# A two-layer spectral and convolutional network on one core: a new order list for the stretch without convolution, and a small column fix-up split into a load and an arithmetic part

## The chip, the core and the metric

The kernel runs on one core of a Trainium2 chip. The core has five engines that matter here: TensorE (PE in the profile; its weight loads are PEld), VectorE (DVE), ScalarE (ACT), GpSimd (POOL) and SyncE (SP), which here only issues DMA transfers. Each engine works through its own queue in order; semaphores tie the queues together. The metric is device time in microseconds (us). Three runs of the kernel before took 4526.14, 4532.66 and 4543.19 us; the profiled run took 4532.45 us, with a span of 4530.7 us from first to last instruction.

## What is computed

The input is `x` of shape (4, 256, 256, 64). Layer 0 does this for each of the four images:

```
h   = layernorm(x) @ w_te + b_te                     # 64 -> 128 channels
F   = fft2(h)                                        # over the 256 x 256 positions
fc  = gelu(concat(real F, imag F) @ w_fc + b_fc)     # 256 -> 256 channels, at each frequency
sp  = real(ifft2(fc[:128] + i fc[128:]))
x1  = x + sp @ w_tp + b_tp
h2  = layernorm(x1) @ w_fe + b_fe
out = x1 + gelu(depthwise_conv3x3(h2, w_dw) + b_dw) @ w_fp + b_fp
```

Layer 1 adds a moving average over the first axis to a filtered spectrum; in the kernel it is a product with one 256 x 256 matrix for each channel. Everything is fp32.

## The kernel before, in words

The forward and inverse Fourier transforms are products with cosine and sine tables. `forward_h` transforms the rows h of the image in chunks of two columns and their mirror images, and writes the result to DRAM (`y_d`). `spectral` transforms along w, mixes channels, applies gelu, projects back and transforms back along w, writing to DRAM (`u_d`). `convolution` transforms back along h, adds the residual, normalises, does the 3x3 convolution by rows and writes `x_d`. A last stage multiplies by layer 1's matrices.

These parts overlap. On TensorE, VectorE, ScalarE and GpSimd the order of instructions is written out by hand: `period(n)` walks a list of short operation names, and `do(op, index)` first does what `FOLLOWS` says must come before. A name with `:-1` means the operation of one index earlier. There are two lists:

- `SPECTRUM`, for periods without convolution: n = 35 to 70, 36 periods, while the first image's spectrum is made.
- `FULL`, for the periods with convolution: n = 71 to 204. Convolution of the four images begins at n = 71, 104, 136 and 169.

One period of `SPECTRUM` handles one forward chunk, two pairs of spectral blocks and one backward step. What the letters are (line numbers are those of the profile):

- forward, one each: `fl` load `xt` (L374 to L379); `fq` squares on ScalarE (L328); `fr`, `fm` two reductions on VectorE (L331, L338); `fR`, `fM` two small VectorE steps (L335, L342); `fp` a power on GpSimd, `rstd` (L348); `fx` scaling on GpSimd (L355); `fa`, `fb` two add/subtract pairs on VectorE (`xb` L392, `xt` L412); `fh0`, `fh1` on GpSimd (`xb` L417); `y0`, `y1` matmuls (L423) with evictions `yt0`, `yt1` on ScalarE (L441). `xb` has one buffer, and `fa` follows both `y` of the chunk before.
- spectral, one for each pair: `x` matmuls (L528) and copy `xs` (L543); `m0`, `m1` mixing matmuls (L552), each into two PSUM banks; `gc0`, `gc1` copy the second bank (L566); `b0`, `b1` add and subtract, reading the first bank (VectorE, L571); `g0`, `g1` gelu on ScalarE (L575); `p0`, `p1` fold on GpSimd (L581); `z` matmuls (L605) and copy `zs` (L613); `w` transposes (L622) and copy `zt` (L632).
- backward, one each: `u` matmuls (L654), `us` copy (L671), `uc` (VectorE, L684 and L685), `uf` (VectorE, L716 in even and L703 in odd steps), then a store to `u_d` (L692).
- convolution: `c0`, `s`, `r0`, `r1`, the statistics `cq` to `cp`, and others. `cm` and `cM` are two statistics steps on VectorE and `cp` a power on GpSimd (L348).
- `cc`, `other_columns`: once for each image it reads the columns w = 0 of `u_d`, does nine small VectorE operations (L785 to L797) and writes three corrected columns to DRAM (`fix_d`). `load_u` (L761, L764) reads them eight periods later and more.

All matmul results go through one pool of eight PSUM banks, which are taken in turn in program order: the ninth taking waits until the first bank's reader is done. A period of `SPECTRUM` takes 18 banks. The tile `sq`, in which `fq` and `cq` leave their squares, has one buffer, and `cc` uses that buffer too. DMA transfers are all issued by SyncE in program order.

Of the kernel before, what the change touches and what calls it, by code (L numbers as in the profile page):

```python
# [11 lines left out]
F32 = mybir.dt.float32  # L12
AF = mybir.ActivationFunctionType
ALU = mybir.AluOpType
# [4 lines left out]
P = 128  # L19
N = 256  # L20
C = 64
# [108 lines left out]
def conv_seq_kernel(ctx: ExitStack, tc: tile.TileContext, a: dict, tables: bass.AP, out: bass.AP):  # L130
    nc = tc.nc
    x = a["x"]
# [4 lines left out]
    shared = ctx.enter_context(tc.tile_pool(name="shared", bufs=1))  # L137
# [6 lines left out]
    def column(ap):  # L144
        return ap.rearrange("(p o) -> p o", o=1)
# [47 lines left out]
    with tc.tile_pool(name="prep", bufs=1) as prep:  # L193

        def load(shape, name, src):
            t = prep.tile(shape, F32, tag=name, name=name)
            nc.sync.dma_start(t, src)
            return t

        w_te = load([C, HID], "w_te", a["w_te"])  # L200
        g1 = load([C, 1], "g1", column(a["g1"]))
        b1 = load([C, 1], "b1", column(a["b1"]))
# [155 lines left out]
    y_ds, u_ds = {}, {}  # L358
# [377 lines left out]
    def convolution(pool):  # L736
# [7 lines left out]
        name = lambda j: f"c_{j[0]}_{j[1]}"  # L744

        fixed, firsts = {}, {}
# [22 lines left out]
        def first_column(j):  # L769
            if j[1] == 0:  # L770
                col = ucs[j][:, 0]
                nc.vector.tensor_tensor(col, col, firsts.pop(j)[:, ::-1], ALU.add)

        def other_columns(j):

            b, q = j
            if q:
                return
            fixed[b] = spill.tile([P, 3, 2, C], F32, tag="fix_d", name=f"fix_d_{b}")
            v = shared.tile([P, 8, 2, C], F32, tag="sq", name=f"fix_{b}")  # L780
            for i in range(2):
                nc.sync.dma_start(v[:, 2 * i : 2 * i + 2], u_ds[b][i][:, :, 0])
            swapped = lambda t: t[:, ::-1]
            tt = nc.vector.tensor_tensor
            tt(v[:, 4], v[:, 2], swapped(v[:, 3]), ALU.add)  # L785
            tt(v[:, 5], v[:, 0], swapped(v[:, 1]), ALU.subtract)
            tt(v[:, 6], v[:, 2], swapped(v[:, 3]), ALU.subtract)
            total, diff = v[:, 0], v[:, 1]
            tt(total, v[:, 5], v[:, 6], ALU.add)
            tt(diff, v[:, 5], v[:, 6], ALU.subtract)  # L790

            tt(v[:, 3, 0], diff[:, 1], total[:, 0], ALU.subtract)
            tt(v[:, 3, 1], diff[:, 0], total[:, 1], ALU.add)
            nc.vector.scalar_tensor_tensor(
                v[:, 5, 0], total[:, 0], -1.0, diff[:, 1], ALU.mult, ALU.subtract
            )
            tt(v[:, 5, 1], total[:, 1], diff[:, 0], ALU.subtract)  # L797
            nc.sync.dma_start(fixed[b], v[:, 3:6])

        def load_x(j):  # L800
            b, q = j
# [40 lines left out]
        tt = pool.tile([P, NP, N + 2], F32, tag="tt", name="tt", bufs=1)  # L842
# [182 lines left out]
        def when(f, is_first):  # L1025
            return lambda j: f(j) if (j[1] == 0) == is_first else None
# [4 lines left out]
            "UL": when(load_u, True),  # L1031
            "XL": when(load_x, True),
            "c0": first_column,
            "cc": other_columns,
            "s": back_h,
            "r0": residual_even,
# [155 lines left out]
    for b in range(B):  # L1192
# [9 lines left out]
        fh0 fb | fh1 fb | y0 fh0 fh1 | y1 fh0 fh1 | yt0 y0 | yt1 y1  # L1202
        xs x m0:-2 m1:-2 | m0 xs | m1 xs | gc0 m0 z:-2 | gc1 m1 z:-2 | b0 gc0 | b1 gc1 | g0 b0 | g1 b1
        p0 g0 | p1 g1 | z p0 p1 | zs z w:-1 | w zs | zt w | us u uc:-1 | uc us uf:-1 | uf uc
        s ul UL c0 | r0 s xl XL | r1 r0 | cq r1 | cr r1 | cR cr | cm cq | cM cm cR | cp cM
        cx cp t0:-1 t1:-1 | t0 cx | t1 cx | tt0 t0 T0:-1 T1:-1 | tt1 t1 T0:-1 T1:-1
        T0 tt0 tt1 eh:-2 | T1 tt0 tt1 gh:-2 | gm T1 | gh gm T1:1 | em T0 | eh em T0:1
        gc_0 gh o1:-2 | gc_1 gh o1:-2 | cf0 gc_0 | cf1 gc_1 | ce0 eh cf0 cf1 | ce1 ce0 | cE ce1
# [4 lines left out]
    def numbered(text):  # L1213

        return [(w.split(":")[0], int(w.split(":")[1]) if ":" in w else 0) for w in text.split()]

    follows = {}
    for line in FOLLOWS.replace("\n", "|").split("|"):
# [4 lines left out]

    FULL = numbered("""
        c0 s cf0:-3 cf1:-3 b0:-1 b1:-1 r0 r1 fx:-1 g0:-1 z:-2 zs:-2 x xs g1:-1 p0:-1 p1:-1
        o0:-4 fs0:-4 o1:-4 fs1:-4 ul:1 cq cr cR cm cM cp t0:-1 tt0:-1 t1:-1 tt1:-1 w:-2 zt:-2
        cx em:-3 eh:-3 T1:-1 T0:-1 fq fr fR fm fM fp m0 gc0 m1 gc1 ce0:-3 ce1:-3 cE:-3
        u us b0 b1 uc z:-1 zs:-1 x:1 xs:1 y0:-2 y1:-2 yt0:-2 yt1:-2 fl:1 a0:-3 a1:-3
        fa:-1 fb:-1 fh0:-1 fh1:-1 ft0:-4 ft1:-4 st0:-4 st1:-4 xl:1 cc w:-1 zt:-1 uf
        g0 g1 p0 p1 gm:-2 gh:-2 gc_0:-2 gc_1:-2 m0:1 gc0:1 m1:1 gc1:1 UL:1 XL:1  # L1230
    """)

    SPECTRUM = numbered("""
        fl:1 p0:-2 fq x z:-2 fr g0:-1 b1:-1 y0:-2 fx:-1 zs:-2 w:-2 fm xs g1:-1 m0 yt1:-2 zt:-2 fa:-1
        m1 u gc1 fR gc0 p0:-1 yt0:-2 fb:-1 us b1 fM p1:-1 b0 x:1 g1 fh1:-1 z:-1 fh0:-1 xs:1 m0:1
        zs:-1 uc gc0:1 w:-1 uf g0 m1:1 zt:-1 b0:1 fp y1:-1 gc1:1 p1
        UL:1 XL:1
    """)
    PAIRS = set("x xs m0 m1 gc0 gc1 b0 b1 g0 g1 p0 p1 z zs w zt".split())
# [45 lines left out]
    with in_order, ExitStack() as right:  # L1285
        with (
            tc.tile_pool(name="fwd", bufs=2, side="left") as fwd,
            tc.tile_pool(name="mix", bufs=2, side="left") as mixing,
        ):
            forward = forward_h(fwd)  # L1290
            load_group, begin, spectrum = spectral(mixing)
            ops |= forward
            do("fl", 0)
            with tc.tile_pool(name="matrices", bufs=2, side="right") as pool:
                m = matrices(pool)
                for n in range(S0):
                    starting(n, m)
                m[1]()
                load_group(0)
                begin(0)  # L1300
            ops |= spectrum
            conv = right.enter_context(tc.tile_pool(name="conv", bufs=2, side="right"))
            ops |= convolution(conv)
            for n in range(S0, S0 + opened(B - 1) + 2):
                period(n)
# [53 lines left out]
```

## Time and profile before

The stages below are from the profile's table of windows; busy times in each window of 100 or 200 us are given as shares of it.

| stretch, us | what runs | PE busy | DVE busy | POOL busy | ACT busy |
|---|---|---|---|---|---|
| 100 to 300 | forward alone, layer 1's matrices | 100% | 74% | 82% | 35% |
| 400 to 800 | the `SPECTRUM` list | 86 to 87% | 98 to 99% | 83 to 85% | 81 to 82% |
| 800 to 1000 | change to `FULL`, image 0 | 80, 86% | 93, 90% | 80, 83% | 71, 58% |
| 1000 to 1700 | the `FULL` list | 100% | 94 to 96% | 78 to 81% | 66 to 69% |
| 1800 to 1900 | change to image 1 | 92% | 92% | 74% | 61% |
| 2600 to 2800 | change to image 2, forward done | 100% | 79% | 54% | 63% |
| 3400 to 3600 | change to image 3 | 95% | 76% | 47% | 39% |
| 4000 to 4530 | end of convolution, layer 1 | 95% | 25% | 3% | 21% |

A busy share by itself doesn't say what a stage waits for; the groups of instructions, the waits and the timeline of the stage do.

### The profile page before, as it was taken

The numbers are of one execution on the slowest core, as the hardware profiler recorded it, in microseconds if no ns is written. First come the engines' busy times: TensorE is split into PE (matmuls) and PEld (weight loads), VectorE is DVE, ScalarE is ACT, GpSimd is POOL, SyncE is SP. The second block draws the span as 40 slices with busy tenths as digits, with TensorE's granted clock in tenths as the row PEclk, the third lists the DMA queues.
The fourth block names the chain that finished last, engine by engine and source line by source line (L and its number), as shares of the span: only waits on it lengthen the run. The fifth ranks groups of instructions, "written<-read, shape, count | busy, mean of one in ns | idle before, by whom it ended". The sixth has DMA issues, their size and how long they took to land.

```text
span 4530.7 us, 63718 instructions
## 1 busy us (share of the span) xinstructions
PE 4348.9 (96%) x22347; PEld 2227.3 (49%) x22347; DVE 3595.4 (79%) x5451; ACT 2506.6 (55%) x3686; POOL 2773.2 (61%) x1806
## 2 busy tenths in 40 slices
PE   7998888889999999999999999999999999999999
PEld 4543333345555555455555555555555455554444
DVE  6778999989999999999999777777777788862222
ACT  2337888666666666666666666666664333331111
POOL 5887888788888777787777555555554555530000
PEclk9999999999999999999999999999999999999999
DMA  5665555434444444444444343333334333328897
GB/s 172 203 191 152 141 144 148 139 105 131 131 131 133 137 127 135 124 135 135 137 137 117 94 117 98 99 107 94 104 107 144 100 101 94 103 89 321 318 327 266
DMA packets 756583, 655.02 MB, mean 145 GB/s; under 512 B 40141, under 2 KB 649375, under 8 KB 747944
## 3 DMA queue, kind: packets, MB, share of 16 engines
q1 hardware_dynamic: 756264, 650.95, 47.6%
q8 instruction: 179, 2.93, 0.3%
q14 instruction: 140, 1.15, 0.1%
HBM read 364.81 MB, written 286.00 MB: 144 GB/s over the span
## 4 chain that ended last, share of the span: by engine, by line
PE 76%; DVE 8%; POOL 4%; issue 2%; DMA 2%; SPq 0%; ACT 0%; POOLq 0%; DVEq 0%; ACTq 0%
PE ps_h_c L897 19%; PE ps_h_c L916 11%; PE ps_o L1156 9%; PE ps_p L552 7%; PE ps_f_c L972 5%; PE ps_s_c L814 4%; PE ps_z L605 4%; PE ps_u L654 4%; PE ps_x L528 4%; PE ps_t_c L851 3%; PE ps_ft_c L993 3%; DVE xb L392 2%; PE ps_y L423 2%; PE ps_zt L622 2%; DVE g L571 2%
## 5 line engine op out<-in xcount | busy, mean ns | idle before, releaser
L581 POOL TENSOR_TENSOR g<-g 128x512 f32<-128x512 f32 (+1 forms) x520 | 710.6, 1377 | 511.7 <-ACT g L575 511.6
L897 PE MATMUL ps_h_c<-td_c,wc_main 128*128 128x512 f32 x2048 | 923.7, 594 | 5.2 <-DVE h_c L942 5.2
L571 DVE TENSOR_TENSOR g<-ps_p,g 128x512 f32<-128x512 f32 x1040 | 693.2, 682 | 27.4 <-ACT g L566 9.3
L575 ACT ACTIVATE g<-g,b_fc 128x1024 f32<-128x1024 f32 (+1 forms) x520 | 586.4, 1148 | 225.5 <-DVE g L571 225.5
L348 POOL TENSOR_TENSOR rstd_c<-var_c,minus_half 128x16 f32<-128x16 f32 x128 | 371.8, 2905 | 475.2 <-DVE var_c L342 464.5
L552 PE MATMUL ps_p<-xs,wp 64*128 64x512 f32 (+1 forms) x2080 | 512.5, 602 | 63.9 <-ACT xs L543 61.6
L566 ACT COPY g<-ps_p 128x512 f32<-128x512 f32 (+1 forms) x520 | 299.6, 585 | 476.9 <-PE ps_p L552 474.1
L897 PEld LDWEIGHTS ps_h_c<-td_c,wc_main 128*128 128x128 f32 x2048 | 369.5, 190 | 376.0 <-issue 303.2
L916 PEld LDWEIGHTS ps_h_c<-td_c,wc_half 64*128 64x128 f32 x4032 | 417.6, 187 | 244.8 <-issue 195.2
L916 PE MATMUL ps_h_c<-td_c,wc_half 64*128 64x128 f32 (+1 forms) x4032 | 516.0, 393 | 3.9 <-POOL td_c L871 3.9
L1156 PE MATMUL ps_o<-xc,mt 128*128 128x512 f32 x1024 | 446.6, 598 | 19.0 <-DMA xc<-x_d 19.0
L348 POOL TENSOR_TENSOR rstd<-var,minus_half 128x16 f32<-128x16 f32 x128 | 373.1, 2915 | 81.9 <-DVE var L342 47.2
L417 POOL TENSOR_TENSOR xb<-xt 128x512 f32<-128x512 f32 x256 | 325.0, 1291 | 158.6 <-DVE xt L412 156.5
L948 DVE TENSOR_TENSOR h_c<-h_c,ps_h_c 128x512 f32<-128x512 f32 x512 | 317.2, 682 | 128.1 <-PE ps_h_c L916 128.0
L965 ACT ACTIVATE h_c<-h_c,b_conv 128x1024 f32<-128x1024 f32 x256 | 280.4, 1146 | 199.6 <-DVE h_c L961 199.6
L1170 DVE TENSOR_SCALAR oc<-ps_o,b_fp 128x512 f32<-128x512 f32 x128 | 96.1, 751 | 367.2 <-PE ps_o L1156 367.2
L941 DVE TENSOR_TENSOR h_c<-h_c,ps_h_c 128x512 f32<-128x512 f32 x256 | 175.7, 686 | 194.7 <-PE ps_h_c L916 186.5
L1156 PEld LDWEIGHTS ps_o<-xc,mt 128*128 128x128 f32 x1024 | 195.6, 192 | 269.2 <-issue 239.7
L605 PE MATMUL ps_z<-g,w_tp 128*64 128x512 f32 x1024 | 281.2, 611 | 40.0 <-POOL g L581 36.6
L528 PEld LDWEIGHTS ps_x<-tab,yb 128*64 128x64 f32 x4064 | 247.8, 139 | 145.9 <-issue 125.2
L552 PEld LDWEIGHTS ps_p<-xs,wp 64*128 64x128 f32 x2080 | 198.8, 187 | 212.7 <-issue 108.0
L1168 ACT ACTIVATE oc<-ps_o,b_fp 128x512 f32<-128x512 f32 x128 | 88.0, 688 | 378.8 <-PE ps_o L1156 270.5
(137 smaller groups left out, 7773.7 us busy)
## 6 DMA issues: line engine op xcount, KB each, us to landing
y_d<-yt SPq DMA_DIRECT2D x256, 256.0 KB, 2.6
yb<-y_d SPq DMA_DIRECT2D x256, 256.0 KB, 3.7
x_c<-in_x_dram SPq DMA_DIRECT2D x128, 512.0 KB, 5.4
u_d<-ut SPq DMA_DIRECT2D x256, 256.0 KB, 4.2
x_d<-st SPq DMA_DIRECT2D x128, 512.0 KB, 4.6
xc<-x_d SPq DMA_DIRECT2D x64, 1024.0 KB, 7.7
out_dram<-oc SPq DMA_DIRECT2D x256, 256.0 KB, 3.2
xt<-in_x_dram SPq DMA_DIRECT2D x504, 128.0 KB, 2.6
```

The source lines that it names most:

```text
L348: nc.gpsimd.tensor_tensor(rstd, var, minus_half.to_broadcast([P, n]), ALU.pow)
L417: nc.gpsimd.tensor_tensor(sums[j][:, i], x0, x1, (ALU.add, ALU.subtract)[i])
L528: nc.tensor.matmul(ps[r * C : (r + 1) * C, j * N + t * P : j * N + (t + 1) * P], blk[:, t, k, r * C : (r + 1) * C], tb[:, t, :], start=Tru ...
L552: nc.tensor.matmul(ps[:, :nf], wp[rows, cols], rhs[rows], start=True, stop=r == 1 or not pr["special"],)
L571: nc.vector.tensor_tensor(gt[:, i], re, gt[:, 1], op)
L575: nc.scalar.activation(g, g, AF.Gelu, bias=b_fc[:, half : half + 1])
L581: nc.gpsimd.tensor_tensor(g[:, 0], g[:, 0], g[:, 1], op)
L605: nc.tensor.matmul(ps[r * C : (r + 1) * C, :nf], w_tp, d[:, :nf], start=True, stop=True)
L897: nc.tensor.matmul(ps, wc_main[:, par, k, :], ts[(*j, k)].rearrange("p j i -> p (j i)"), start=True, stop=False,)
L916: nc.tensor.matmul(pss[k, par][:, s * P : (s + n) * P], wc_half[lo : lo + C, k, :], ts[(*at_q, k)][lo : lo + C, at : at + n, :].rearrange( ...
L948: nc.vector.tensor_tensor(g, g, m, (ALU.add, ALU.subtract)[r])
L1156: nc.tensor.matmul(ps[:, :nf], mts[i // CM][:, i % CM, t, to * P : (to + 1) * P], xc[:, t, :, :, i, :], start=t == 0, stop=t == 1,)
```

## The change

Two things are changed. First, the text of `SPECTRUM` is replaced by another order of the same operations. Second, the load of the columns w = 0 becomes an operation of its own, `cl`, at the place where `cc` was in `FULL`, with a tile of its own (`raw`, one buffer, 2 KB in each partition); the arithmetic, still `cc`, comes one period later, right after `cM`, and is rearranged so that its three results lie in `raw` and the temporaries in the `sq` buffer. The aim is that VectorE doesn't reach the arithmetic before its data is there, and that the stretch without convolution runs in a better order.

```diff
+        def load_columns(j):
+            b, q = j
+            if q == 0:
+                raw = firsts[b] = pool.tile([P, 4, 2, C], F32, tag="raw", name=f"raw_{b}", bufs=1)
+                for i in range(2):
+                    nc.sync.dma_start(raw[:, 2 * i : 2 * i + 2], u_ds[b][i][:, :, 0])
+
         def other_columns(j):
...
-            v = shared.tile([P, 8, 2, C], F32, tag="sq", name=f"fix_{b}")
-            for i in range(2):
-                nc.sync.dma_start(v[:, 2 * i : 2 * i + 2], u_ds[b][i][:, :, 0])
+            t = shared.tile([P, 8, 2, C], F32, tag="sq", name=f"fix_{b}")
...
-            nc.sync.dma_start(fixed[b], v[:, 3:6])
+            nc.sync.dma_start(fixed[b], raw[:, 0:3])
...
-        s ul UL c0 | r0 s xl XL | r1 r0 | cq r1 | cr r1 | cR cr | cm cq | cM cm cR | cp cM
+        cc cl | s ul UL c0 | r0 s xl XL | r1 r0 | cq r1 | cr r1 | cR cr | cm cq | cM cm cR | cp cM
...
-        o0:-4 fs0:-4 o1:-4 fs1:-4 ul:1 cq cr cR cm cM cp t0:-1 tt0:-1 t1:-1 tt1:-1 w:-2 zt:-2
+        o0:-4 fs0:-4 o1:-4 fs1:-4 ul:1 cq cr cR cm cM cc:-1 cp t0:-1 tt0:-1 t1:-1 tt1:-1 w:-2 zt:-2
...
-        fa:-1 fb:-1 fh0:-1 fh1:-1 ft0:-4 ft1:-4 st0:-4 st1:-4 xl:1 cc w:-1 zt:-1 uf
+        fa:-1 fb:-1 fh0:-1 fh1:-1 ft0:-4 ft1:-4 st0:-4 st1:-4 xl:1 cl w:-1 zt:-1 uf
...
     SPECTRUM = numbered("""
-        fl:1 p0:-2 fq x z:-2 fr g0:-1 b1:-1 y0:-2 fx:-1 zs:-2 w:-2 fm xs g1:-1 m0 yt1:-2 zt:-2 fa:-1
-        m1 u gc1 fR gc0 p0:-1 yt0:-2 fb:-1 us b1 fM p1:-1 b0 x:1 g1 fh1:-1 z:-1 fh0:-1 xs:1 m0:1
-        zs:-1 uc gc0:1 w:-1 uf g0 m1:1 zt:-1 b0:1 fp y1:-1 gc1:1 p1
+        fr m0:-1 x g1:-1 xs p1:-1 gc0:-1 x:1 fq m0 z:-2 b0:-1 y1:-2 xs:1 fm gc0 m1 fR zs:-2 g0:-1
+        gc1 w:-2 fx:-1 fl:1 y0:-2 fM zt:-2 b0 p0:-1 fp z:-1 fa:-1 fb:-1 yt1:-2 fh1:-1 u b1 yt0:-2
+        zs:-1 us fh0:-1 uc m1:1 w:-1 g0 gc1:1 b1:1 p0 zt:-1 g1 p1 uf
         UL:1 XL:1
     """)
```

With what `FOLLOWS` forces, a steady period's queues come out like this:

```
VectorE before  fr b1:-1 fm fa:-1 fR fb:-1 b1 fM b0 uc uf b0:1
VectorE after   fr b0:-1 fm fR fM b0 fa:-1 fb:-1 b1 uc b1:1 uf
GpSimd before   p0:-2 fx:-1 p0:-1 p1:-1 fh1:-1 fh0:-1 fp p1
GpSimd after    p1:-1 fx:-1 p0:-1 fp fh1:-1 fh0:-1 p0 p1
ScalarE before  fq g0:-1 zs:-2 xs g1:-1 yt1:-2 zt:-2 gc1 gc0 yt0:-2 us g1 xs:1 zs:-1 gc0:1 g0 zt:-1 gc1:1
ScalarE after   g1:-1 xs gc0:-1 fq xs:1 gc0 zs:-2 g0:-1 gc1 zt:-2 yt1:-2 yt0:-2 zs:-1 us g0 gc1:1 zt:-1 g1
TensorE before  x z:-2 y0:-2 w:-2 m0 m1 u x:1 z:-1 m0:1 w:-1 m1:1 y1:-1
TensorE after   m0:-1 x x:1 m0 z:-2 y1:-2 m1 w:-2 y0:-2 z:-1 u m1:1 w:-1
```

## The prediction

> **What bounds the kernel now.** I read the table of windows first, to see which engine is full in which stretch.
>
> ```profile
> 500.00:600.00 100.00, 86.17 (x552) 36.87 (x550) 98.64 (x132) 81.12 (x123) 84.22 (x55) 1.00 0.52 144
> 1200.00:1300.00 100.00, 100.00 (x581) 52.72 (x578) 94.47 (x144) 66.03 (x97) 78.97 (x50) 1.00 0.48 137
> 2620.00:2640.00 20.00, 20.00 (x113) 11.18 (x113) 15.17 (x25) 11.75 (x18) 11.61 (x8) 1.00 0.28 79
> ```
>
> Columns: window, its length, busy us of PE, PEld, DVE, ACT and POOL, then granted clock, DMA share and GB/s. Under `SPECTRUM` (first row) DVE is full at 98.6% and PE is not; under `FULL` (second row) PE is full. The third row is the change to image 2: PE is full there too.
>
> Next, what fills DVE under `SPECTRUM`: the groups by shape, 450 to 850 us, and the timeline of one period.
>
> ```profile
> L571 DVE TENSOR_TENSOR g<-ps_p,g 128x512 f32<-128x512 f32 x214 | 146.8, 686 | 4.4 <-ACT g L566 0.7
> L392 DVE TENSOR_TENSOR xb<-xt 128x512 f32<-128x512 f32 x54 | 83.9, 1593 | 1.9 <-PE ps_y L423 0.7
> L412 DVE TENSOR_TENSOR xt<-xb 128x512 f32<-128x512 f32 x52 | 34.7, 709 | 0.0
> ...
> 555.16 1.28 POOL L581 TENSOR_TENSOR g<-g 128x512 f32<-128x512 f32 x1
> 556.78 1.34 POOL L581 TENSOR_TENSOR g<-g 128x512 f32<-128x512 f32 x1 [0.34 <-ACT g L575]
> ...
> 555.46 3.21 DVE L392 TENSOR_TENSOR xb<-xt 128x512 f32<-128x512 f32 x2
> 558.71 1.29 DVE L412 TENSOR_TENSOR xt<-xb 128x512 f32<-128x512 f32 x2
> 564.04 1.23 DVE L716 TENSOR_TENSOR ut<-ut,ut 128x1024 f32<-128x1024 f32 x1
> 562.63 2.91 POOL L348 TENSOR_TENSOR rstd<-var,minus_half 128x16 f32<-128x16 f32 x1
> ```
>
> L392 and L412 are the same operation by size, yet L392 takes 1593 ns and L412 709. The timeline says why: while GpSimd folds (L581), L392 stands; each of its two instructions ends 0.55 us after one of the folds (558.67 after 558.12 for the second). So full DVE time holds a wait that counts as busy: 3.21 - 1.29 = 1.92 us in a period. L571, with one input in PSUM, isn't slowed, and neither is L716 beside GpSimd's power L348. The same `xb` pair comes every 14.67 us (from 394.9 to 804.8, 28 periods).
>
> Last, the waits and the PE timeline where convolution of an image begins.
>
> ```profile
> DVE fix L785 <- DMA fix<-u_d: 10.9, 1, 10.9
> ...
> 1816.67 1.98 PE L605 MATMUL ps_z<-g,w_tp 128*64 128x512 f32 x4 [3.41 <-DVE h_c L942]
> ...
> 3509.75 1.88 PE L897 MATMUL ps_h_c<-td_c,wc_main 128*128 128x512 f32 x4
> 3516.79 3.78 PE L897 MATMUL ps_h_c<-td_c,wc_main 128*128 128x512 f32 x4 [5.17 <-DVE h_c L942]
> ```
>
> At image 3 the fix-up's load sits behind 6 MB of layer-1 loads (4 of 1024 KB, 4 of 512 KB), DVE stands 10.9 us and PE 5.17 us; the next four matmuls take twice as long (3.78 against 1.88).
>
> **What the Trainium skill says.** "GPSIMD Engine Reference", Specifications: GpSimd shares its SBUF interfaces with VectorE and contends with VectorE instructions that have two SBUF inputs. The trace agrees, with one refinement: the folds block, the power (16 elements) doesn't. "VectorE: DVE Perf Modes", the section on the TRN2 errata, gives (N+151)/0.96 ns for an fp32 tensor_tensor: 691 for 512 elements, against 682 to 691 unblocked here. "TensorE: Matmul & The Clock Gate", Part 1: after an idle window of about 3.4 us the clock halves. The two rows above agree.
>
> **Part 1, the fix-up.** No instruction or transfer is added; `cl` carries the two loads that `cc` had. Nine operations of 0.21 to 0.29 us make 2.0 us when free.
>
> - Image 0: they ran from 896.51 to 904.06, 7.55 us, each waiting on a fold of GpSimd, and DVE is 98% busy there. In the new place, between `cM` and `fr`, GpSimd goes on to `cp`, a power, which doesn't block. Gain 5.5 us.
> - Image 1: 1807.63 to 1813.99, 6.4 us; behind them on DVE stood L941/L942, which PE waited for: 3.41 us, then cold matmuls (z 1.98, x 1.95, f 2.81 against 1.08, 1.04, 1.89): 2.7 us. Gain 6.
> - Image 2: PE is full, gain 0.
> - Image 3: the load now has a whole period (26 to 28 us) to land; rows of L782 land in 2.5 us, the bad one in about 7. PE's 5.17 us go, and about 3.5 us of cold matmuls (3.78, 2.61, 2.97 against 1.88, 2.00, 1.94). Gain 8.5 to 9.
>
> What queues behind `cc` now is `fr` (forward) or `cf0`/`ce0`; at 2 us in a DVE that is 95% busy I cost it at nothing, because PE's own queue, full in row two, hides it. `fq` waits for `cc` to leave `sq`, a period's slack. Sum 21 us; bounds 10 (images 1 and 3 give only PE's idle time, 8.6, and image 0 little) and 28.
>
> **Part 2, the list.** The same operations, so engine sums stay: a period has 12.70 us of PE, 12.28 of POOL, 11.93 of ACT, and 14.46 of DVE, of which 1.92 is blocking. What decides is who waits for whom. I laid one new period out by hand with the durations of the rows. Zero is the end of the last period's `b1:1`.
>
> ```
>  0.00  b1:1 ends (DVE). g1:-1, then xs on ACT; m0 starts at 1.71
>        (same chain before: DVE pair ends 561.33, matmul starts 563.04)
>  1.71  PE in order: m0 1.06, z 0.91, y1 0.91, m1 1.06, w 0.59
>  6.24  y0 starts, ends 1.08 later, 7.32
>  7.44  fa may start (xb has one buffer; 0.12 us after y0 as before)
>  9.87  fa, fb done at 2.43 us, if GpSimd is in its power then
> 11.28  b1 ends (1.41); frees the bank that m1:1's second half takes
> 12.04  that matmul alone ends (0.07 + 0.69)
> 12.73  gc1:1 ends (0.10 + 0.59)
> 14.19  b1:1 ends (0.05 + 1.41): one period
> ```
>
> The bank follows from the rotation: m1's first bank is the 9th taken in a period, m1:1's second the 17th, eight later. Beside this chain, GpSimd: p1 (1.05 to 2.3, after `uf` lets go), p1:-1 to 3.55, fx to 5.4, p0:-1 6.13 to 7.4 (its gelu ends at 6.05), power 7.4 to 10.25, so `fa` and `fb` do run beside the power and the 1.92 us are gone; fh to 12.7, p0 to 13.95, before `uf` at 14.1. `fR` at 4.66 waits on fx until 5.4, but `b0` still ends (7.1) before `fa` may start. DVE so gets about 0.65 us of new idle time (before `fa` and `b1:1`) and 0.8 of blocking in place of 1.92. Gain 14.67 - 14.19 = 0.48 us for 28 periods, 13 us; the first periods and the four after the special group (19.4, 15.4, 13.8, 13.6 us apart before) I take as even.
>
> Forecast: 4532.7 - 21 - 13 = 4498.7, say 4498.
>
> **Rivals.**
>
> - *The list reaches its floor* (0.15). If my links are too long, GpSimd and the lock bound it: POOL 12.28 + `uf`'s 1.14 that can't lie beside the power = 13.4. 28 x 1.27 = 36; with 21 that is 4476. For it: before, two periods late in the stretch took 13.8 and 13.6. Against: the wait of `fa` on `y0`.
> - *The list gives nothing* (0.20): one link 0.5 us longer (gelu g0 stands ahead of gc1:1 on ACT and ends at about 12.04 too), period 14.67. Only the fix-up counts: 4512.
> - *One lock wait more* (0.07): p0:-1 gets in ahead of `fM`, 0.5 us apart in my layout, and a fold of 1.25 us enters the chain: 15.45. 28 x 0.78 = 22 lost, 21 won: 4533.
> - *A second standing wait*, slower (0.08): `uf` and the late p1 push each other as well, 16.7 us. 28 x 2.03 = 57 lost: 4569. The tightness of these near-ties speaks for it, DVE's slack against it.
>
> **How the numbers follow.** Forecast 0.50. Its 20 us of size error put it over the 0.5% line (4510) in 0.43; with the floor 0.15 and the part of "nothing" with a large fix-up gain, 0.12, faster has 0.70. Slower is the last rival, 0.08; the rest, 0.22, is within 0.5%. The range goes from just below the floor case to "nothing" with a small fix-up gain: 4472 to 4522, leaving out the last two rivals and a little of the floor.
>
> **What would show it.** L392's mean under `SPECTRUM` falls from 1593 to about 700 ns, and the power of `fp` lies beside it; the spacing of `xb` pairs is 14.0 to 14.4 us, with DVE idle before `xb` ended by `ps_y`; `raw` has no DMA wait on DVE; PE's 5.17 and 3.41 us are gone; the image-2 change is as before. It is wrong if L335/L342 or `ut` take over the blocking, if the spacing isn't below 14.67, or if PE idles as much where images change.

## The result and the profile after

| kernel | us, median (range) | ratio to before, 95% interval |
|---|---|---|
| before | 4532.94 (4526.14 to 4543.19) | |
| after | 4496.51 (4494.40 to 4502.32) | 0.992 [0.990, 0.994] |

The change saves 36.4 us, 0.8%; 4498 was predicted. That number hides more than it shows, so the gain is followed through the kernel. The trace gives a mark that both kernels pass 128 times: the start of `r0` of each chunk under convolution (L827 before, L833 after). The lead of after over before at these marks:

| stretch | lead of after, us | step |
|---|---|---|
| `c0` of the first chunk | 24.0 | |
| `r0` of the first chunk | 18.4 | -5.6 |
| steady in image 0 | 24.1 | +5.7 |
| steady in image 1 | 27.4 | +3.3 |
| start of image 2 | 27.4 | 0 |
| steady in image 3 | 34.3 | +6.9 |
| first output matmul `ps_o` | 34.3 | 0 |
| end of the profiled execution | 31.2 | -3.1 |

The last row isn't the change's doing: from the first `ps_o` to the end the profiled kernels took 466.8 to 476.4 us with the same code, 470.4 in before and 473.5 in after. A lead at `ps_o` is therefore the better measure of an edit, and a difference of 2 or 3 us between two medians here is none.

A lead counted from the start of the profile also holds what happened before the first chunk. In the forward stage, where every kernel still runs the code of before, after leads by 0.07 us, while the experiments' kernels are 0.3 to 2.6 us behind (the 21st `xb` pair of each, at about 221 us). The tables of the experiments count the lead from there, so that in them after has 24.0, 27.3 and 34.2 us. Five kernels with the same code up to the first chunk under convolution then lead by 23.9 to 24.3 us at its `c0`: counted so, a lead from one profile is good to about 0.5 us.

The window of one new period under `SPECTRUM`, from one `xb` pair to the next; the columns are those of the windows of before.

```profile
561.94:575.88 13.94, 13.05 (x82) 5.22 (x84) 13.22 (x20) 11.88 (x19) 13.21 (x9) 1.00 0.54 152
```

The period is 13.94 us, not 14.67. VectorE is busy 13.22 us of it, no longer nearly all of it, and GpSimd is as full as VectorE. The groups by shape from 430 to 830 us say what VectorE was spared:

```profile
L392 DVE TENSOR_TENSOR xb<-xt 128x512 f32<-128x512 f32 x56 | 36.2, 687 | 15.3 <-PE ps_y L423 15.3
L335 DVE SCALAR_TENSOR_TENSOR var<-total 128x16 f32<-128x16 f32 x28 | 20.9, 747 | 0.0
```

L392 has fallen from 1593 to 687 ns, which is the mean of L412 too (687 ns). In its place stand two smaller losses: 15.3 us of idle time ahead of L392 that TensorE's `y0` ends, and L335, 747 ns for 16 elements, which now stands beside GpSimd's scaling, `fx`. The timeline of the period, VectorE and then GpSimd:

```profile
561.93 1.29 DVE L392 TENSOR_TENSOR xb<-xt 128x512 f32<-128x512 f32 x2 [0.51 <-PE ps_y L423]
...
573.06 0.77 DVE L335 SCALAR_TENSOR_TENSOR var<-total 128x16 f32<-128x16 f32 x1
...
561.77 2.90 POOL L348 TENSOR_TENSOR rstd<-var,minus_half 128x16 f32<-128x16 f32 x1
...
571.88 1.92 POOL L355 TENSOR_TENSOR xt<-xt,rstd 128x1024 f32<-128x1024 f32 x1
```

`fa` and `fb` lie beside the power, L348, as forecast. L335 stands from 573.06 to 573.83, and the GpSimd multiplication L355 ends at 573.80.

### The profile page after: what moved, and what is told of

Same layout as the page of the kernel before. It is cut to its first block, busy times and chain, and to the rows that moved or that the text cites. A ratio compares the mean times of both kernels' runs of the same rounds, so it can differ in the third digit from the quotient of the medians.

```text
span 4499.5 us, 63495 instructions
## 1 busy us (share of the span) xinstructions
PE 4360.6 (97%) x22347; PEld 2221.8 (49%) x22347; DVE 3546.6 (79%) x5451; ACT 2504.6 (56%) x3686; POOL 2800.8 (62%) x1806
## 4 chain that ended last, share of the span: by engine, by line
PE 85%; POOL 5%; DMA 3%; DVE 3%; issue 2%; ACT 1%; SPq 0%; POOLq 0%; DVEq 0%; ACTq 0%
PE ps_h_c L903 19%; PE ps_h_c L922 11%; PE ps_o L1163 9%; PE ps_p L552 8%; PE ps_z L605 5%; PE ps_f_c L978 5%; PE ps_u L654 5%; PE ps_s_c L820 5%; PE ps_y L423 4%; PE ps_x L528 4%; PE ps_t_c L857 3%; PE ps_ft_c L999 3%; POOL xb L417 2%; PE ps_zt L622 2%; PE ps_m L1101 2%
## 5 line engine op out<-in xcount | busy, mean ns | idle before, releaser
L581 POOL TENSOR_TENSOR g<-g 128x512 f32<-128x512 f32 (+1 forms) x520 | 737.3, 1431 | 522.1 <-ACT g L575 522.0
L348 POOL TENSOR_TENSOR rstd_c<-var_c,minus_half 128x16 f32<-128x16 f32 x128 | 371.8, 2905 | 467.3 <-DVE var_c L342 456.6
L348 POOL TENSOR_TENSOR rstd<-var,minus_half 128x16 f32<-128x16 f32 x128 | 372.9, 2913 | 84.4 <-DVE var L342 48.3
L605 PE MATMUL ps_z<-g,w_tp 128*64 128x512 f32 x1024 | 281.0, 611 | 21.9 <-POOL g L581 20.4
```

What stands on the lines that cost most here:

```text
L348: nc.gpsimd.tensor_tensor(rstd, var, minus_half.to_broadcast([P, n]), ALU.pow)
L581: nc.gpsimd.tensor_tensor(g[:, 0], g[:, 0], g[:, 1], op)
L605: nc.tensor.matmul(ps[r * C : (r + 1) * C, :nf], w_tp, d[:, :nf], start=True, stop=True)
```

## The experiments

The theory was the prediction's: two independent gains, the list's (a blocked VectorE replaced by a shorter chain through `y0`) and the fix-up's (blocked arithmetic in image 0, PE's waits in images 1 and 3). The rivals were that one of the two does nothing, and that what blocks VectorE isn't GpSimd.

### Each half alone

The list alone: the changed kernel with load and arithmetic of w = 0 as before. The fix-up alone: the changed kernel with the old `SPECTRUM`.

```diff
-        ... xl:1 cl w:-1 zt:-1 uf             (list alone: cc as before, with its loads)
+        ... xl:1 cc w:-1 zt:-1 uf
...
-        fr m0:-1 x g1:-1 xs p1:-1 ...         (fix-up alone: old text of SPECTRUM)
+        fl:1 p0:-2 fq x z:-2 fr g0:-1 ...
```

> The kernel before with the new SPECTRUM list alone; the column fix-up stays as it was. Theory (the list's gain is the blocked time of L392 that goes, 14.67 to 13.94 us a period, and the fix-up at image 0 was worth little): the first chunks of convolution run 24 us earlier than before, as in the changed kernel, images 1 and 3 show no further gain; time about 4509. Rival (the 24 us at image 0 hold 5.5 us of the fix-up, as the prediction had it): only 18.5 us earlier after image 0; time about 4514.

> The changed kernel with the old SPECTRUM list: the fix-up's change alone. Theory: 0 to 1 us at image 0, 3 us at image 1, 0 at image 2, 7 us at image 3: about 10 us, 4522. Rival (the prediction's 5.5 us at image 0 are real and add to the others): about 16 us, 4517. A third: image 0 loses and takes back part of it: 4526 or more.

| lead, us | list alone | fix-up alone | after |
|---|---|---|---|
| image 0 | 19.0 | 3.4 | 24.0 |
| image 1 | 21.1 | 6.7 | 27.3 |
| image 3 | 20.4 | 13.2 | 34.2 |

The list alone takes 4516.0 us (0.9963 [0.9949, 0.9977]), the fix-up alone 4517.96 (0.9967 [0.9955, 0.9979]). Both count. For the list alone the rival came true: 19 us in image 0, not 24. For the fix-up alone the lead of 13.2 us lies between the theory (10) and its rival (16). The list gives more than the 13 us of the prediction, the fix-up less than the 21: 13.2 with the old list, and 34.2 - 20.4 = 13.8 on top of the new one. So over the whole kernel the two add. Image by image they don't quite: in image 0 the fix-up is worth 3.4 us under the old list and 5.0 under the new.

### The wait on y0

In the new list `fa` waits for `y0:-2`, the last but one of TensorE's queue. The experiment moves it right behind `y1:-2`.

```diff
-        ... b0:-1 y1:-2 xs:1 ...
+        ... b0:-1 y1:-2 y0:-2 xs:1 ...
...
-        gc1 w:-2 fx:-1 fl:1 y0:-2 fM ...
+        gc1 w:-2 fx:-1 fl:1 fM ...
```

> The changed kernel with one name moved in SPECTRUM: y0 directly after y1, so before m1 and w on TensorE (1.65 us earlier). Theory (the period of 13.94 is a chain through fa's wait for y0, DVE idle 0.51 us before fa): the wait goes, and the period falls to what VectorE needs with its blocking, 13.4 us; 28 to 30 periods of 0.5 us, 15 us, about 4482. Rival (the interface shared by VectorE and GpSimd bounds the period, and fa's wait is only where its slack shows): period stays at 13.9, same time. Second rival: m1, 0.9 us later, makes gc1 and b1 late: period about 14.3, time about 4506.

It took 4490.95 us (0.9911 [0.9897, 0.9924]); by time that can't be told from after. The spacing of the `xb` pairs alternates, 13.34 and 14.30 us, 13.82 in the mean against 13.94. VectorE's timeline over two of its periods:

```profile
562.53 1.29 DVE L392 TENSOR_TENSOR xb<-xt 128x512 f32<-128x512 f32 x2
...
575.88 1.62 DVE L392 TENSOR_TENSOR xb<-xt 128x512 f32<-128x512 f32 x2
...
582.71 1.75 DVE L716 TENSOR_TENSOR ut<-ut,ut 128x1024 f32<-128x1024 f32 x1
```

The idle time before L392 is gone in both periods, and the time comes back as blocking in every second one: L392 1.62 us instead of 1.29, L716 1.75 where after has 1.25. So the wait on `y0` was a real limit, but the next one is right behind it, and most of the 0.5 us that the theory expected of the spacing is given back (13.82 in the mean, not 13.4). What is left shows in the lead: 22.9 us at the last `xb` pair of the list's steady part, where after has 19.9, and 37.1 against 34.2 at the first `ps_o`.

### What blocks VectorE

Five small blocks of twelve VectorE instructions of 128x512 were put at the start of the changed kernel, each beside six GpSimd instructions of one kind (or none). The comments in the cut say what the kinds are.

```diff
+            for _ in range(6):
+                on_pool[g]()      # none | gc = ga + gb | gq = gp ** -0.5 (16 wide)
+            for _ in range(12):
+                on_dve[d]()       # lc = la + lb | lc = lps (PSUM) + lb | sum of la
```

> The changed kernel with five blocks of independent instructions ahead of everything else, on tiles of their own; in each VectorE runs twelve instructions on 512 elements and GpSimd six beside them: (1) two SBUF inputs, GpSimd idle; (2) two SBUF inputs beside GpSimd adds with two SBUF inputs; (3) one input in PSUM beside the same adds; (4) a reduction (one input) beside the same adds; (5) two SBUF inputs beside GpSimd's power on 16 elements. Theory (two-input instructions of the two engines exclude each other, by turns): VectorE 0.69 us in 1, 1.8 to 1.9 us in 2 as long as GpSimd has work, with GpSimd's adds also 1.8 to 1.9; 0.69 in 3, 0.65 in 4, 0.69 in 5. Rival (they share bandwidth, whatever the operands): 2 and 3 alike, each engine slowed in proportion, 4 less. Second rival (any GpSimd instruction blocks): 5 shows 2.9 us waits too.

The blocks as VectorE's timeline has them, and below them GpSimd's; L184 is the add of two SBUF tiles, L185 has one input in PSUM, L186 is the sum, L190 GpSimd's add, L191 its power.

```profile
7.52 8.75 DVE L184 TENSOR_TENSOR lc<-la,lb 128x512 f32<-128x512 f32 x12
...
26.94 14.34 DVE L184 TENSOR_TENSOR lc<-la,lb 128x512 f32<-128x512 f32 x12
...
44.19 8.67 DVE L185 TENSOR_TENSOR lc<-lps,lb 128x512 f32<-128x512 f32 x12
...
66.41 8.68 DVE L184 TENSOR_TENSOR lc<-la,lb 128x512 f32<-128x512 f32 x12
...
6.63 18.33 POOL L191 TENSOR_TENSOR gq<-gp,minus_half 128x16 f32<-128x16 f32 x6
...
26.26 10.11 POOL L190 TENSOR_TENSOR gc<-ga,gb 128x512 f32<-128x512 f32 x6
```

GpSimd's powers need nothing of the blocks before, so they ran first, beside VectorE's first twelve adds, and the last twelve had GpSimd idle: 8.75 us beside the powers, 8.68 without. Beside GpSimd's adds the same twelve take 14.34. While both run they alternate: in the trace each VectorE add then takes 1.63 us instead of 0.69 and each GpSimd add 1.59 instead of 1.26, with a new one on each engine every 1.67 us. That is less than the 1.8 to 1.9 us expected: the two don't quite pay for each other's whole time (0.69 + 1.26 = 1.95). With one input in PSUM VectorE isn't slowed (8.67), nor in the sum (7.88 for eleven), and GpSimd's adds take 1.26 us there, all but the first. So neither rival holds. This is the cause that the prediction read from one timeline, now by itself: adds with two SBUF inputs on the two engines go by turns, while GpSimd's power, small as it is, lets VectorE pass.

### Place or load

The fix-up moves the arithmetic and also brings the load forward. One kernel keeps the early load and puts the arithmetic back at the old place, one period later; the other keeps the new place and issues the load right ahead of it.

```diff
-        ... cM cc:-1 cp ...      xl:1 cl w:-1      (early load, old place)
+        ... cM cp ...            xl:1 cl cc:-1 w:-1
...
-        ... cM cc:-1 cp ...      xl:1 cl w:-1      (new place, own load)
+        ... cM cl:-1 cc:-1 cp ...   xl:1 w:-1
```

> The changed kernel with the load of the raw columns where the change puts it, but the arithmetic of w = 0 back at the old place, ahead of w:-1, zt:-1 and uf, one step later so that it has its data. It separates the early load from the new place. Theory: the early load alone takes away VectorE's wait for the transfer (about 7 us, in image 3), and the new place alone is worth the 5.7 us in image 0; so the lead over the kernel before is about 19 us in image 0, 21 us after image 1 and 27 us at the first output matmul. Rival: the place doesn't matter, the lead is that of the changed kernel, 24.1, 27.4 and 34.3 us.

> The changed kernel with the arithmetic of w = 0 at the place the change gives it, but with its load issued right ahead of it, not one step earlier. It is the new place without the early load. Theory: VectorE now waits for the transfer at each of these places, 2 to 3 us or more, so image 0 keeps about half of its 5.7 us (lead 20 to 22 us against 24.1) and image 3 loses its 7 us (lead about 27 us at the first output matmul). Rival: the transfer is hidden at the new place, since VectorE has a queue of older work there: lead as in the changed kernel, 24.1 and 34.3 us.

The time the nine operations took from first to last in each image, taken from the trace, us, and the leads, counted from the forward stage (at the first `ps_o` they are within 1.5 us of those in image 3; the two new kernels have one run each):

| kernel | image 0 | 1 | 2 | 3 | lead in image 0, 1 | lead in image 3 |
|---|---|---|---|---|---|---|
| list alone | 7.62 | 6.46 | 1.86 | 1.89, after a DMA wait of 11.7 | 19.0, 21.1 | 20.4 |
| early load, old place | 1.75 | 6.43 | 1.75 | 2.75 | 23.7, 27.1 | 31.3 |
| new place, own load | 1.79 | 1.79 | 1.79 | 8.11, DMA wait of 2.0 inside | 24.5, 27.8 | 30.3 |
| after | 1.79 | 1.79 | 1.79 | 2.19 | 24.0, 27.3 | 34.2 |

Neither expectation holds whole. In images 0 and 1 each kernel keeps the gain, as the rivals had it: in image 0 the old place one period later happens to lie beside a power of GpSimd, and at the new place the transfer is hidden even when issued right ahead. In image 3 each loses 3 to 4 us, as the theories had it in kind. Only after has all four images short. Image 3 shows why both parts are wanted. With its own load there, first VectorE and then GpSimd:

```profile
3489.02 0.29 DVE L793 TENSOR_TENSOR fix<-raw 128x128 f32<-128x128 f32 x1 [1.96 <-DMA raw<-u_d]
...
3489.95 1.95 DVE L798 TENSOR_TENSOR raw<-fix 128x64 f32<-128x64 f32 x1
3491.81 1.07 DVE L799 TENSOR_TENSOR raw<-fix 128x64 f32<-128x64 f32 x1
...
3489.91 1.90 POOL L355 TENSOR_TENSOR xn_c<-x_c,rstd_c 128x1024 f32<-128x1024 f32 x1
3491.77 1.04 POOL L877 TENSOR_TENSOR td_c<-tt 128x512 f32<-128x512 f32 x1
```

The DMA wait itself is 1.96 us. It pushes the arithmetic past the end of `cp`'s power, which lets VectorE pass, and L798 stands through the whole of GpSimd's L355, 1.95 us for 64 elements; then the two go by turns. In after the wait is 0.34 us and the arithmetic is through before the power ends:

```profile
3486.68 0.29 DVE L793 TENSOR_TENSOR fix<-raw 128x128 f32<-128x128 f32 x1 [0.34 <-DMA raw<-u_d]
```

Image 1 says something else: with the early load at the old place the nine operations still take 6.43 us, and its lead still grows by 3.4 us there, as in after (3.3). So the blocking itself cost nothing there that the change could win back.

### The joint between the two lists

The new list leaves `m0:-1` and `gc0:-1` at the start of the next period. Where `FULL` takes over, at n = 71, they come behind `s`. First TensorE and VectorE in after, then VectorE's `c0`:

```profile
855.21 3.78 PE L820 MATMUL ps_s_c<-uc_c,tab 64*128 64x512 f32 x8 [5.12 <-DVE uc_c L772]
...
860.80 1.42 DVE L571 TENSOR_TENSOR g<-ps_p,g 128x512 f32<-128x512 f32 x2 [5.69 <-ACT g L566]
...
853.76 1.35 DVE L772 TENSOR_TENSOR uc_c<-uc_c,first 128x128 f32<-128x128 f32 x1
```

TensorE stands 5.12 us for `c0` with `m0:-1` queued behind `s`, VectorE 5.69 us for the copy of what `m0:-1` makes, and `s` runs at half speed (3.78 us for eight, 2.02 at the change to image 1). This is where the table of leads drops by 5.6 us. The experiment puts the two entries ahead:

```diff
-        c0 s cf0:-3 cf1:-3 b0:-1 ...
+        m0:-1 gc0:-1 c0 s cf0:-3 cf1:-3 b0:-1 ...
```

> The changed kernel with one more reordering: at the joint n = 71 the three entries m0:-1, gc0:-1 and b0:-1's predecessors go ahead of s in the list FULL instead of behind it. In the changed kernel TensorE waits 5.12 us there for the first c0 and VectorE 5.69 us for gc0, and the lead of the first chunk falls from 24.0 us (at c0) to 18.4 us (at its r0). Theory: the wait is the price of entries that were left behind s, so with them ahead of s the lead of chunk 0 is about 5 us larger in image 0 and once more after it where the joint recurs, and the whole takes about 4491 us (4488 to 4495). Rival: s needs c0 in any case and c0 itself comes no earlier, so the entries moved only change who waits: at most 1 us, 4496 us.

> The changed kernel with the joint reordered as in the run before this one and y0:-2 moved directly behind y1:-2 in the stretch without convolution. Theory: the two gains lie at different places (5 us at the joint, about 5.5 us over the stretch), so they add: about 4485 us (4482 to 4490). Rival: the earlier stretch is handed back at the joint, where c0 is what everything waits for: 4491 us, as with the moved y0 alone.

Leads are again counted from the forward stage.

| kernel | us | ratio to before | lead at first `r0`, image 0, image 3 |
|---|---|---|---|
| after | 4496.51 | 0.992 [0.990, 0.994] | 18.3, 24.0, 34.2 |
| joint mended | 4495.93 | 0.9906 [0.9890, 0.9923] | 22.3, 27.8, 38.0 |
| joint mended and `y0` early | 4497.42 | 0.9913 [0.9898, 0.9928] | 24.3, 29.5, 39.7 |
| `y0` early | 4490.95 | 0.9911 [0.9897, 0.9924] | 21.1, 24.9, 37.1 |

```profile
855.23 3.32 PE L820 MATMUL ps_s_c<-uc_c,tab 64*128 64x512 f32 x8 [4.06 <-issue]
...
858.51 1.22 DVE L833 TENSOR_TENSOR x_c<-x_c,ps_s_c 128x1024 f32<-128x1024 f32 x1 [2.06 <-PE ps_s_c L820]
```

With the joint mended VectorE's wait falls to 2.06 us, and the lead is 4.0 us larger at the first `r0` and 3.8 in images 0 and 3: by the lead the cause is shown, and the size was put at 5. `c0` itself comes no earlier (853.78), so TensorE still stands 4.06 us. The two edits nearly add: in image 3 the mended joint brings 3.8 us, the earlier `y0` 2.9 and both together 5.5. The rival, that the joint hands back what the earlier `y0` wins, isn't borne out: the first `c0` is 26.7 us ahead of before with both edits and 24.2 with the joint alone.

The times show none of this. All four kernels beat before, but none can be told from after, and 4495.93 us is what the rival of the first run expected. In the profiled execution of both edits 2.6 us were lost before the forward stage's mark and 2.9 behind the first `ps_o`, where the edits change nothing. Whether those losses are chance, one profile of each kernel doesn't say.

## Why the prediction was right, and where it was wrong

The number was right (34 us of gain by its sum, a lead of 34.3 us at `ps_o`), and so was the mechanism in its main part: `xb` freed from GpSimd's folds, the fix-up's arithmetic beside GpSimd's power, and the early load in image 3. That the sum fits within 2 us is luck. The list gave 20.4 us where 13 was put, the fix-up 13.8 on top of it where 21 was put (its items make 20 to 20.5): two misses of some 7 us with opposite signs.

- **L392 freed beside the power: right.** About 700 ns predicted, 687 measured. The list alone has 688, and the separate blocks show the cause by itself.
- **The chain from `b1:1` to `fa`: right.** From the end of `b1:1` to `m0` 1.71 us was predicted and 1.71 measured, to `fa` 7.44 and 7.48. The idle time before `fa` and L335's 0.8 us of blocking are there (0.51, 0.77). Taking away the wait on `y0` shows that it was a limit, not the only one.
- **"frees the bank that m1:1's second half takes": wrong.** In the list's term this is the step that failed. I had taken the eight PSUM banks in a fixed turn, as the section on the kernel before says too, so that `m1:1` would wait for `b1`. TensorE's and VectorE's timelines, with `m1:1` first and `b1` below:

```profile
564.58 1.13 PE L552 MATMUL ps_p<-xs,wp 64*128 64x512 f32 x4
...
564.47 1.41 DVE L571 TENSOR_TENSOR g<-ps_p,g 128x512 f32<-128x512 f32 x2
```

All four matmuls of `m1:1` end at 565.71, before `b1` ends at 565.88. The bank numbers in the program built from the kernel follow no fixed turn: `m1:1` gets the second bank of `m1`, which `gc1` empties, and the bank of `w:-2`. In place of that link stands VectorE's own queue: after `b1` come the two instructions of `uc` and then `b1:1`, without idle time. `b1:1` ends 2.52 us after `b1`, not 2.91, and the period is 13.94, not 14.19. The saving is 0.73 us a period: over the 27 spacings from the start of the steady part to its end the lead of the `xb` pairs grows from 0.1 to 20.0 us, against 13 predicted.

- **First periods and change of list taken as even: wrong at the joint.** 5.6 us are lost there, of which mending it brings 3.8 to 4.0 back. The prediction laid out a steady period and didn't follow the entries left over to the next list.
- **Image 0, gain 5.5: about right**: 24.0 - 19.0 = 5.0 us on top of the new list. With the old list it is 3.4; why less, was not tried.
- **Image 1, gain 6: wrong, the largest miss of the sum.** After leads by 27.3 - 21.1 = 6.2 us over the list alone, of which 5.0 were there in image 0: 1.2 us. With the old list the fix-up gave 6.7 - 3.4 = 3.3. TensorE's waits in 80 us around the change to image 1, before and then after:

```profile
PE ps_z L605 <- DVE h_c L942: 3.4, 1, 3.4
PE ps_z L605 <- POOL g L581: 2.6, 2, 2.5
```

```profile
PE ps_z L605 <- POOL g L581: 3.8, 2, 3.6
PE ps_u L654 <- DVE h_c L954: 1.2, 2, 0.9
PE ps_y L423 <- DVE g L571: 0.5, 1, 0.5
```

The wait of 3.4 us that I counted is gone, as forecast, but others grew: for GpSimd's folds from 2.6 to 3.8, for VectorE 0.3 to 1.2, and 0.5 new. Removing the wait that ended last uncovered those behind it: between the 29th and the 45th `r0` TensorE's idle time falls by 1.0 us only, from 8.5 to 7.5. Its busy time falls by 2.4 us, close to the 2.7 of cold matmuls (those that take up to twice as long after a wait) that I had counted. But the list alone already brings that, 2.7 us, and 2.1 us of the 3.3 by which the lead of after grows here, so little of it was left for the fix-up.

- **Image 2, nothing: right**: the lead is 27.3 us in image 1 and in image 2.
- **Image 3, gain 8.5 to 9: too large.** 7.6 us against the list alone, 6.9 within after. PE's 5.17 us are gone, but I took the waits and cold matmuls behind them wrongly. Before, and then after in two parts:

```profile
3527.15 2.97 PE L972 MATMUL ps_f_c<-h_c,w_fp 128*64 128x512 f32 x8 [1.10 <-ACT h_c L965]
```

```profile
3492.35 1.07 PE L978 MATMUL ps_f_c<-h_c,w_fp 128*64 128x512 f32 x2 [1.53 <-ACT h_c L971]
3493.61 1.93 PE L978 MATMUL ps_f_c<-h_c,w_fp 128*64 128x512 f32 x6 [0.18 <-ACT h_c L971]
```

Of the 3.5 us of cold matmuls this 1 us stays: the eight take 3.00 us in after, 2.97 before. The wait ahead of them grows from 1.1 to 1.7 us and that for `td_c` from 3.9 to 4.3. Together that leaves 5.17 + 2.5 - 1.0 = 6.7 us.

Of the marks that the prediction named, `raw` has one DMA wait of 0.34 us instead of none, and the spacing lies just under its 14.0 to 14.4 us; the others came as said. Of its signs of being wrong one came in part: around the change to image 1 TensorE's waits only fall from 6.3 to 5.5 us. "GPSIMD Engine Reference", Specifications, in the Trainium skill says that GpSimd contends with VectorE instructions with two SBUF inputs; the separate blocks agree (14.34 us beside it, 8.68 without, 8.67 with one input in PSUM).

## What to carry to other kernels

Busy time of VectorE that exceeds the same operation elsewhere (here 1593 against 687 ns) can hold a wait: look at what GpSimd does beside it, and put GpSimd's long small operations beside VectorE's two-input work and its folds beside work with an input in PSUM. Price a new order list with the change to the next list included, since the joint cost 5.6 us here, as much as eight periods gain, and entries left over there were most of it. When kernels are compared by marks in a trace, take off what they already differ by where their code is still the same (up to 2.6 us here). A wait removed where several engines are nearly even is worth only the distance to the next one: look up that one before counting it.

## What the runs showed of the hardware that was not expected

The blocking goes both ways, and a short instruction can stand through the whole of a long one: a 64-element VectorE instruction of 0.22 us took 1.95 us beside one GpSimd multiplication of 1.90. GpSimd's adds slow from 1.26 to 1.59 us while VectorE's go from 0.69 to 1.63. GpSimd's power on 128x16, though one takes 2.9 to 3.5 us, slows VectorE by less than 1% (8.75 against 8.68 us for twelve adds).
